# Four fused convolution layers on one core: the first batch's x in quarters of channels, weights on another queue, and reordered steps at the start, in the attention rounds and in the last blocks

## The chip, the core and the metric

The kernel runs on one core of a Trainium2 chip. TensorE (PE in the profile) does the matrix products, VectorE (DVE), ScalarE (ACT) and GpSimd (POOL) do the elementwise work, SyncE (SP) issues the transfers. The metric is the device time of one execution in microseconds. The kernel before takes 2680.13 us (median of three runs, 2679.41 to 2680.3). The profile used below is of one further execution, with a span of 2676.2 us on the core and a mean granted TensorE clock of 0.999.

## The reference, cut to what matters

An input x of shape (4, 512, 64, 64) in float32 goes through four layers, each of which adds to its input:

- layer 0, attention over the 4096 positions of an image with 64 channels: `scores = key^T query`, a softmax over the keys, `out = value @ attn`, then `scale * (w_out @ out) + x`. key, query and value are 1x1 convolutions of x by one weight array of 192 x 512.
- layer 1, a bottleneck of three convolutions (1x1, 3x3, 1x1) whose weights are mixed from eight experts; the mixing factors are a sigmoid of a linear map of the mean of layer 0's output.
- layer 2, linear attention: softplus features of Q and K, `KV = K V^T`, a division by a norm.
- layer 3, two projections of 512 to 512 channels; one is summed along columns and rows with a discount per channel, and the sigmoid of it multiplies the other.

The softmax in the kernel subtracts no maximum. The kernel collects the inverse sums of the exponentials and tests at run time that all lie in a range; a flag `fits` says so, and a slower general program behind a branch runs if they don't.

## The kernel before

**Tiling.** Channels are the 128 partitions in KC = 4 quarters. The 4096 positions are cut in four pieces of 1024 (a "pair" of two blocks of 512), and x[pr] holds all 512 channels of piece pr. All products are float32. The profile records a product of 512 columns as two matmul records; where two products of 64 output rows run side by side on the two halves of the array, as in most of layer 0, a group "x8" is two such pairs over two quarters.

**Start (L99 to L159).** SyncE issues the weights `wqkv` (L100, 128 x 4 pieces of 768 bytes), the parameters `prm` (L102), then x: pieces 0 and 1 in four transfers of one quarter of the channels each (L93, 512 KB), pieces 2 and 3 as one transfer each (L95, 2 MB). Up to eight transfers are under way at a time, because each uses one of eight semaphores in turn and the ninth waits for the first.

**First stage (`Projections`, L213 to L337).** TensorE's order is the program's order (the PE schedule is manual), and so is that of DVE and ACT in this stage. Pieces are taken in twos, (0, 1) and (2, 3). Keys and queries of the two pieces are made with seven products instead of eight (a Strassen-like scheme, numbered 1 to 7), written in the strings of `steps` (L230). What the words of a string mean:

- `v1`: the value product of piece 1 over all four quarters; `v3a`, `v3b` its halves.
- `1` to `7`: a product over two quarters (`kq`, `kqz`, L305); 1, 6, 7 and 4 accumulate in one bank, which is copied out on the way (`seed`, `e2`, `e3`, ACT, L310 and L313) or at the end (`c21`, DVE). 2 accumulates on the seed and needs channels 2 and 3 of the first piece only.
- `t5`, `n5` and so on: the sums of x that 4, 5, 6 and 7 need (DVE, L253), of this pair or the next.
- `c11` (ACT, L291): four copies of product 2's result to `key`. `c22`, `c12`: DVE additions into `qry` and `key`. `k`: the second copy of the keys that `c12` made.
- `cp01`, `tr01`: the values to SBUF (ACT), turned by TensorE, and copied (DVE).
- `zero`: a product of identities that has no use but to occupy the array and to clear a bank.

All products of one pair's scheme that go to `zy` share one PSUM tile; product 3 is written after `c11` and `c22` have read it. PSUM has three such double tiles (`pair_psum`) and two single banks (`bank`).

**Rounds (L458 to L481).** Attention goes over 128 steps i = (pr, kt), pr the query piece and kt the tile of 128 keys. A round g is eight `scores` (PE, L367, then the exponential on ACT, L370, and its sum into `acc` on DVE, L375) and eight `values` (PE, L382), which run four steps behind the scores. There are 16 rounds. `late` is a list of work for finished query pieces: `sums(pr)` is the sum over partitions (PE `den`, L398), its reciprocal (DVE, L401), the scaled result (L410, L412) and two range reductions (L419, L420); `out_step(pr, m)` is an output product (PE `y`, L426) and its addition to x (DVE, L431). At the end of each round up to two items of the list are taken:

```python
for _ in range(2):
    if late and late[0][0] <= g:
        late.pop(0)[1]()
```

For the last query piece `inverse_sums(3)` (`den` and its reciprocal) is put in by hand before the step `done == 121` of the values, seven before the end (L456).

**Layers 1 to 3.** Layer 1 mixes the weights and does `conv1` (L567), `sums_of_six`, `conv2` (L616), `conv3`. In layer 3 a `Block` is a set of seven products (L920); `Sums` blocks are summed along rows (`rows`, L953), turned (`turn`, ACT, L959), summed along columns (L970), and go through a sigmoid (L976); `Gates` blocks multiply by them, add x (L1015) and send the result out (L1017). The step tables `steps`, `last_steps` and, for the last two gates of the last batch, `end_steps` (L1037) say which step of which block comes when: s is the sums block, g and h the gates blocks, l the sums block before.

**Flag (L1114 to L1123).** After the last batch DVE reduces the collected inverse sums, TensorE adds up the partitions (`cnt`, L1122) and DVE casts the result to `fits` (L1123). Every engine then loads `fits` and branches (L1514, L1515).

Of the kernel before, what the change touches and what calls it, by code (L numbers as in the profile page):

```python
# [8 lines left out]
F32 = mybir.dt.float32  # L9
# [6 lines left out]
P = 128  # L16
# [5 lines left out]
D = 64  # L22
# [24 lines left out]
def unshifted(ctx: ExitStack, tc: tile.TileContext, fits, x, wqkv_t, wout_t, router_t,  # L47
# [16 lines left out]
    def bank(name, shape=(P, NB)):  # L64
        return ps.tile(list(shape), F32, tag="acc", name=name)
# [20 lines left out]
    def load_pair(b, pr):  # L86
        if b and pr == NPAIR - 1:
            places[NPAIR - 1:] = places[NPAIR], places[NPAIR - 1]
        t = places[pr]
        src = x[b, :, pr * 2 * NB:(pr + 1) * 2 * NB].rearrange("(kc p) n -> p kc n", p=P)  # L90
        if b == 0 and pr < 2:
            for kc in range(KC):
                nc.sync.dma_start(t[:, kc, :], src[:, kc, :])  # L93
        else:
            nc.sync.dma_start(t, src)  # L95
        return t


    wqkv_sb = const.tile([P, KC, 3 * D], F32, tag="wqkv", name="wqkv_sb")  # L99
    nc.sync.dma_start(wqkv_sb, wqkv_t.rearrange("(kc p) o -> p kc o", p=P))  # L100
    prm_sb = const.tile([P, NPRM], F32, tag="prm", name="prm_sb")
    nc.sync.dma_start(prm_sb, prm)  # L102
    def col(i, n=1):
        return prm_sb[:, i:i + n]

# [107 lines left out]
    class Projections:  # L213
# [14 lines left out]
            nc.vector.tensor_tensor(self.w[3], a12, self.w[6], ALU.subtract)  # L228

        def steps(self, b):  # L230
            first = "v1 cp01 5 1 seed v2 t6 t4 n5 6 n6 e2 2 7 e3 c22 c11 tr01 n7 4 c21 3 c12 n4"
            if b == 0:
                first = "zero v0 1 seed t5 v1 cp01 t6 5 2 t7 t4 6 e2 v2 7 e3 n5 c22 c11 tr01 n6 n7 4 c21 3 c12 n4"
            return first.split(), "5 1 seed k v3a 6 e2 2 v3b cp23 7 e3 c22 c11 tr23 4 c21 3 c12".split()

        def key_copies(self):
            while self.left:
# [44 lines left out]
        def products(self, xs, pair, steps, key, qry, vt):  # L282
            y = zy = None
            e = {}

            def to_key(src, pr, own=True):
                for h in range(2):
                    n0 = (2 * pr + h) * NB
                    for to in range(2):
                        if own or to != h:  # L290
                            nc.scalar.copy(key[to * D:(to + 1) * D, n0:n0 + NB], src(h, n0))  # L291

            for step in steps:
                if y is None and (step.isdigit() or step == "zero"):
                    y, zy = bank(f"kq_{self.b}_{pair[0]}"), pair_psum(f"kqz_{self.b}_{pair[0]}")
                if step == "zero":

                    nc.tensor.matmul(zy[:, 0, :].rearrange("p (j c) -> p j c", c=P), ident,
                                     ident[:, None, :].to_broadcast([P, TPB, P]), start=True, stop=True)
                elif step.isdigit():  # L300
                    k = int(step)
                    to = y if k in (1, 6, 7, 4) else zy[:, 0 if k == 2 else 1, :]
                    for c in range(2):
                        for h in range(2):
                            nc.tensor.matmul(to[h * D:(h + 1) * D, :], self.w[k][:, c, :],  # L305
                                             self.term(xs, pair, k, c)[:, h * NB:(h + 1) * NB],
                                             start=c == 0 and k in (1, 5), stop=c == 1,
                                             skip_group_check=k not in (1, 5))
                elif step == "seed":
                    nc.scalar.copy(zy[:, 0, :], y)  # L310
                elif step in ("e2", "e3"):
                    e[step] = block(f"{step}_{self.b}_{pair[0]}")
                    nc.scalar.copy(e[step], y)  # L313
                elif step == "c11":
                    to_key(lambda h, n0: zy[h * D:(h + 1) * D, 0, :], pair[0])
                elif step == "c12":
                    for h in range(2):
                        r, n0 = slice(h * D, (h + 1) * D), (2 * pair[1] + h) * NB
                        nc.vector.tensor_tensor(key[r, n0:n0 + NB], zy[r, 1, :], e["e2"][r, :], ALU.add)
                    self.left.append(lambda: to_key(lambda h, n0: key[h * D:(h + 1) * D, n0:n0 + NB], pair[1],  # L320
                                                    own=False))
                elif step == "k":
                    self.key_copies()
                elif step == "c21":
                    nc.vector.tensor_copy(qry[:, pair[0] * NB:(pair[0] + 1) * NB], y)
                elif step == "c22":
                    nc.vector.tensor_tensor(qry[:, pair[1] * NB:(pair[1] + 1) * NB], zy[:, 1, :], e["e3"], ALU.add)
                elif step[0] in "tn" and step[1].isdigit():
                    for c in range(2):
                        self.sum(xs, pair if step[0] == "t" else (2, 3), int(step[1]), c)  # L330
                elif step[:2] == "cp":
                    self.value_copy(int(step[2]) // 2)
                elif step[:2] == "tr":
                    self.value_turn(int(step[2]) // 2, vt)
                elif step[2:] == "a" or step[2:] == "b":
                    self.value(xs, int(step[1]), 0 if step[2] == "a" else 2, 2)
                else:  # L337
                    self.value(xs, int(step[1]))

    def layer0(b, xs, pro):  # L340
# [130 lines left out]
        assert not late  # L471


# [394 lines left out]
    def layer3(b, xs, value_product, value_add, left, weights, wcq):  # L868
# [109 lines left out]
        class Gates(Block):  # L978
# [32 lines left out]
            def add_x(self, i, h=None):  # L1011
# [25 lines left out]
        end_steps = (("s1", "s seed", "l rows 1", "l rows 0"), ("g1", "l turn 1", "g seed"),  # L1037
# [66 lines left out]
                    nxt.append(load_pair(b + 1, i // 2 - 1))  # L1104
        return nxt, pro

    with tc.manual_schedule(engines={mybir.EngineType.PE}):
# [7 lines left out]
    nc.vector.tensor_reduce(ends[:, 0:1], stat[:, 0, :], AX.X, ALU.add)  # L1115
    nc.vector.tensor_reduce(ends[:, 1:2], stat[:, 1, :], AX.X, ALU.min)
    fit = small.tile([P, 2], F32, tag="fit", name="fit", bufs=1)
    nc.vector.tensor_scalar(fit[:, 0:1], ends[:, 0:1], 1.0 / SUM_LO, None, ALU.is_le)
    nc.vector.tensor_scalar(fit[:, 1:2], ends[:, 1:2], 1.0 / SUM_HI, None, ALU.is_ge)
    nc.vector.tensor_tensor(fit[:, 0:1], fit[:, 0:1], fit[:, 1:2], ALU.mult)  # L1120
    cnt = bank("cnt", (1, 2))
    nc.tensor.matmul(cnt, fit[:, 0:1], ones[:, 0:2], start=True, stop=True)  # L1122
    nc.vector.tensor_copy(fits, cnt)  # L1123


@with_exitstack
def general(ctx: ExitStack, tc: tile.TileContext, x, wqkv_t, wout_t, router_t,
                experts, packed, wqk_t, wv_t, bv, wproj_t, prm, out):
# [23 lines left out]


    wqkv_sb = const.tile([P, KC, 3 * D], F32, tag="wqkv", name="wqkv_sb")
    nc.scalar.dma_start(wqkv_sb, wqkv_t.rearrange("(kc p) o -> p kc o", p=P))
# [411 lines left out]
```

## Time and profile before

| what | value |
|---|---|
| time, three runs | 2680.13 us (2679.41 to 2680.3) |
| span of the profiled execution | 2676.2 us, granted TensorE clock 0.999 |
| DVE busy | 2016.3 us (75%) |
| ACT busy | 1314.3 us (49%) |
| scores, L367 | 2048 records, 460.1 us busy |
| value products of the rounds, L382 | 1344 + 704 records, 302.2 + 159.6 us busy |
| layer 3 products, L920 | the chain of waits puts 14% on `sx` and 10% on `zy` |
| x's transfers, L95 | 14 of 2048 KB, 8.6 us to landing (median); the two of the first batch 14.6 and 19.3 us |
| x's transfers, L93 | 8 of 512 KB, 4.5 to 10.2 us to landing |

A row of the timeline has the start in us, the time from the first start to the last end of the merged instructions, the engine, the line, what is written and read, the number of records, and in brackets how long the engine was idle before and what ended it. The ends of matmuls are modelled, so that a group's printed time overlaps the next group's start; the differences of starts say what a group cost. In the list of waits a row has the total in us, how many times, and the longest.

### The profile page before, as it was taken

What the parts mean: (1) busy time and instruction counts of PE and PEld (TensorE: products, weight loads), DVE (VectorE), ACT (ScalarE), POOL (GpSimd) and SP (SyncE); (2) the same over time, 40 slices, a digit from 0 to 9 for tenths busy, and PEclk for the clock granted to TensorE, in tenths of its full rate; (3) what the DMA queues carried; (4) which work ended last, traced back from release to release, by engine and by line L of the source; (5) the groups of instructions that cost most, each with busy time, mean ns of one, the idle gap of its engine ahead of it and who ended that gap; (6) DMA issues with size and microseconds to landing.
All of it is one profiled execution on the core that took longest, in us unless ns stands there. A gap on an engine that the chain in (4) does not pass through costs nothing.

```text
span 2676.2 us, 25813 instructions
## 1 busy us (share of the span) xinstructions
PE 2643.2 (99%) x10048; PEld 1114.9 (42%) x10048; DVE 2016.3 (75%) x2272; ACT 1314.3 (49%) x1510; POOL 12.9 (0%) x26
## 2 busy tenths in 40 slices
PE   8999999999999999999999999999999999999998
PEld 2333364344333345434433334543443333554443
DVE  6777766788777776688877778668886777856787
ACT  3655353455555435345455553535555555263545
POOL 1000000000000000000000000000000000000000
PEclk9999999999999999999999999999999999999999
DMA  5000210022200021002220002101121000210001
GB/s 191 1 1 1 102 32 1 16 110 79 79 1 1 1 102 32 1 33 93 79 79 1 1 1 102 32 1 63 63 87 71 0 1 15 88 32 1 32 40 57
DMA packets 34883, 115.17 MB, mean 43 GB/s; under 512 B 3008, under 2 KB 12224, under 8 KB 33216
## 3 DMA queue, kind: packets, MB, share of 16 engines
q1 hardware_dynamic: 34752, 113.43, 11.4%
q8 instruction: 81, 1.33, 0.2%
q14 instruction: 50, 0.41, 0.1%
HBM read 79.86 MB, written 33.55 MB: 42 GB/s over the span
## 4 chain that ended last, share of the span: by engine, by line
PE 81%; DVE 11%; ACT 3%; issue 2%; DMA 1%; DVEq 0%; SPq 0%; ACTq 0%
PE av L382 14%; PE sx L920 14%; PE s L367 13%; PE zy L920 10%; DVE acc L375 4%; PE z L664 4%; PE c L639 4%; PE c L567 4%; PE c L616 3%; PE wv L838 2%; PE g L740 2%; PE xtr L725 2%; PE y L426 2%; PE c2e L616 2%; PE kqz L305 1%
## 5 line engine op out<-in xcount | busy, mean ns | idle before, releaser
L367 PE MATMUL s<-qv,key 64*128 64x512 f32 x2048 | 460.1, 596 | 0.9
L370 ACT ACTIVATE ring<-s 128x1024 f32<-128x1024 f32 x336 | 316.7, 1048 | 252.9 <-PE s L367 252.5
L375 DVE TENSOR_TENSOR acc<-acc,ring 128x1024 f32<-128x1024 f32 x312 | 381.7, 1223 | 59.2 <-ACT ring L370 31.3
L382 PE MATMUL av<-ring,qv 128*64 128x512 f32 x1344 | 302.2, 595 | 0.0
L367 PEld LDWEIGHTS s<-qv,key 64*128 64x128 f32 x2048 | 190.7, 186 | 265.3 <-issue 128.6
L920 PE MATMUL sx<-t,x 128*128 128x512 f32 x512 | 238.2, 599 | 2.2 <-ACT e L929 2.2
L375 DVE TENSOR_TENSOR acc<-acc,x 128x1024 f32<-128x1024 f32 x168 | 205.5, 1223 | 31.6 <-ACT x L370 15.5
L370 ACT ACTIVATE x<-s 128x1024 f32<-128x1024 f32 x176 | 167.1, 1053 | 124.9 <-PE s L367 124.6
L382 PEld LDWEIGHTS av<-ring,qv 128*64 128x64 f32 x1344 | 92.6, 137 | 200.1 <-issue 200.1
L925 ACT COPY zy<-sx 128x512 f32<-128x512 f32 x64 | 36.5, 570 | 258.0 <-PE sx L920 248.4
L382 PE MATMUL av<-x,qv 128*64 128x512 f32 x704 | 159.6, 595 | 0.0
L920 PEld LDWEIGHTS sx<-t,x 128*128 128x128 f32 x512 | 94.7, 190 | 134.1 <-issue 121.5
L970 DVE TENSOR_TENSOR_SCAN t<-x,t 128x512 f32<-128x512 f32 x128 | 149.2, 1209 | 1.6
L959 ACT COPY t<-s 128x1024 f32<-128x1024 f32 x64 | 127.6, 1993 | 43.9 <-DVE s L953 43.4
L953 DVE TENSOR_TENSOR_SCAN s<-wc,s 128x512 f32<-128x512 f32 x128 | 146.1, 1203 | 1.7 <-ACT s L945 1.7
L929 ACT ACTIVATE e<-sx,prm_sb 128x512 f32<-128x512 f32 x128 | 86.9, 686 | 107.0 <-PE sx L920 106.9
L976 ACT ACTIVATE s<-t 128x1024 f32<-128x1024 f32 x64 | 125.8, 1988 | 11.1 <-DVE t L970 11.1
L920 PE MATMUL zy<-t,wq 128*128 128x512 f32 x256 | 118.5, 602 | 0.5 <-ACT s L938 0.5
L920 PE MATMUL sx<-t,wq 128*128 128x512 f32 x256 | 117.0, 597 | 1.3 <-ACT e L929 1.3
L920 PE MATMUL sx<-x,wq 128*128 128x512 f32 x256 | 117.1, 595 | 0.0
L920 PE MATMUL zy<-x,x 128*128 128x512 f32 x256 | 116.3, 594 | 0.0
L920 PE MATMUL zy<-x,wq 128*128 128x512 f32 x256 | 115.9, 592 | 0.0
(227 smaller groups left out, 3451.1 us busy)
## 6 DMA issues: line engine op xcount, KB each, us to landing
out_dram<-s SPq DMA_DIRECT2D x62, 512.0 KB, 2.6
x<-in_x_dram SPq DMA_DIRECT2D x14, 2048.0 KB, 8.6
ex<-in_packed_dram SPq DMA_DIRECT2D x4, 2048.0 KB, 7.3
ex<-in_experts_dram SPq DMA_DIRECT2D x4, 2048.0 KB, 7.8
wq<-in_wproj_t_dram SPq DMA_DIRECT2D x32, 256.0 KB, 4.8
ex<-in_packed_dram SPq DMA_DIRECT2D x4, 1536.0 KB, 6.0
ex<-in_experts_dram SPq DMA_DIRECT2D x4, 1536.0 KB, 6.5
x<-in_packed_dram SPq DMA_DIRECT2D x4, 1536.0 KB, 7.6
```

The lines of the kernel that those rows point to most:

```text
L367: nc.tensor.matmul(s[:, h, :], key[r, kt * P:(kt + 1) * P], qry[r, pr * NB:(pr + 1) * NB], start=True, stop=True)
L370: nc.scalar.activation(p, s, AF.Exp)
L375: nc.vector.tensor_tensor(accs[pr], accs[pr], p, ALU.add)
L382: nc.tensor.matmul(avs[pr][h * D:(h + 1) * D, :], vt[:, kt, :], ring[i % RING][:, h, :], start=kt == 0, stop=kt == NT - 1)
L567: nc.tensor.matmul(y[:, h, :], wc[:, kc, :], xs[pr][:, kc, h * NB:(h + 1) * NB], start=kc == 0, stop=kc == KC - 1)
L616: nc.tensor.matmul(y[:, lo - a:hi - a], u, v[:, lo:hi], start=dy == 1, stop=dy == 2)
L639: nc.tensor.matmul(y[:, h, :], wc[:, KC + 9 + m, :], h2[:, h, :], start=True, stop=True)
L920: nc.tensor.matmul(y, w[:, c, self.kind, self.j * P:(self.j + 1) * P], v[:, c, :], start=c == 0 and k in (1, 5), stop=c == 1, skip_group_c ...
L953: nc.vector.tensor_tensor_scan(self.half(i, h), along[:, self.j + 2 * i, :], self.half(i, h), 0.0, ALU.mult, ALU.add)
L959: nc.scalar.copy(self.t[i].rearrange("p (w r) -> p w r", w=W), self.s[i].rearrange("p (r w) -> p w r", w=W))
L970: nc.vector.tensor_tensor_scan(th, down[:, i, :], th, 0.0, ALU.mult, ALU.add)
L976: nc.scalar.activation(self.s[i].rearrange("p (r w) -> p w r", w=W), tw, AF.Sigmoid)
```

## The change

It has six parts. They are meant to start TensorE earlier, to take waits off it, and to shorten the work after its last product.

1. All x of the first batch comes in quarters of channels, 16 transfers. `wqkv` and `prm` are issued by ACT instead of SyncE, and `wqkv` lies in memory as the tile does, 3072 bytes to a partition.
2. The identity product `zero` is done twice, and the first pair's products of the first batch follow the quarters as they come.
3. In all batches `c11` comes directly after product 2, and product 2 comes earlier; in the second pair `k` goes to the end.
4. One item of `late` per round instead of two; `inverse_sums(3)` five steps before the end instead of seven.
5. In `end_steps` the two turns of the last sums block come after the copies that the products wait for.
6. The range test is done in layer 1 of the last batch.

```diff
-        if b == 0 and pr < 2:
+        if b == 0:
             for kc in range(KC):
                 nc.sync.dma_start(t[:, kc, :], src[:, kc, :])
...
-    nc.sync.dma_start(wqkv_sb, wqkv_t.rearrange("(kc p) o -> p kc o", p=P))
+    nc.scalar.dma_start(wqkv_sb, wqkv_t)
     prm_sb = const.tile([P, NPRM], F32, tag="prm", name="prm_sb")
-    nc.sync.dma_start(prm_sb, prm)
+    nc.scalar.dma_start(prm_sb, prm)
...
-            first = "v1 cp01 5 1 seed v2 t6 t4 n5 6 n6 e2 2 7 e3 c22 c11 tr01 n7 4 c21 3 c12 n4"
+            first = "v1 cp01 5 1 seed v2a t6 2 c11 t4 n5 6 v2b e2 n6 7 e3 c22 tr01 n7 4 c21 3 c12 n4"
             if b == 0:
-                first = "zero v0 1 seed t5 v1 cp01 t6 5 2 t7 t4 6 e2 v2 7 e3 n5 c22 c11 tr01 n6 n7 4 c21 3 c12 n4"
-            return first.split(), "5 1 seed k v3a 6 e2 2 v3b cp23 7 e3 c22 c11 tr23 4 c21 3 c12".split()
+
+                first = ("zero v0:0 1:0 v0:1 1:1 seed v0:2 2:0 v0:3 2:1 c11 t5 v1:0 v1:1 5 t6 v1:2 v1:3 cp01 t7 6 e2 "
+                         "v2:0 v2:1 t4 7 e3 c22 tr01 n5 4 c21 n6 3 c12 n7 v2:2 v2:3 n4")
+            return first.split(), "5 1 seed v3a 2 c11 6 v3b e2 cp23 7 e3 c22 tr23 k 4 c21 3 c12".split()
...
-                    nc.tensor.matmul(zy[:, 0, :].rearrange("p (j c) -> p j c", c=P), ident,
-                                     ident[:, None, :].to_broadcast([P, TPB, P]), start=True, stop=True)
+
+                    for _ in range(2):
+                        nc.tensor.matmul(zy[:, 0, :].rearrange("p (j c) -> p j c", c=P), ident,
+                                         ident[:, None, :].to_broadcast([P, TPB, P]), start=True, stop=True)
...
-                    if done == NPAIR * NT - 7:
+                    if done == NPAIR * NT - 5:
                         inverse_sums(NPAIR - 1)
...
-                for _ in range(2):
-                    if late and late[0][0] <= g:
-                        late.pop(0)[1]()
+                if late and late[0][0] <= g:
+                    late.pop(0)[1]()
...
-        end_steps = (("s1", "s seed", "l rows 1", "l rows 0"), ("g1", "l turn 1", "g seed"),
-                     ("s6", "s copy_out 2", "l columns 1"), ("s2", "l turn 0", "s first"),
-                     ("s7", "s copy_out 3", "l columns 0", "l sigmoid 1"), ("s5", "s fourth"),
+        end_steps = (("s1", "s seed", "l rows 1", "l rows 0"), ("g1", "g seed"),
+                     ("s6", "s copy_out 2", "l turn 1", "l columns 1"), ("s2", "s first"),
+                     ("s7", "s copy_out 3", "l turn 0", "l columns 0", "l sigmoid 1"), ("s5", "s fourth"),
...
+    def all_in_range():
+
+        ends = small.tile([P, 2], F32, tag="ends", name="ends", bufs=1)
...
             convs = layer1(b, xs, *layer0(b, xs, pro))
+            if b == B - 1:
+                all_in_range()
             xs, pro = layer3(b, xs, *layer2(b, xs, *convs))
-
-
-    ends = small.tile([P, 2], F32, tag="ends", name="ends", bufs=1)
...
-        "wqkv_t": a["L0_conv_w_qkv"].T,
+
+        "wqkv_t": a["L0_conv_w_qkv"].T.reshape(KC, P, 3 * D).transpose(1, 0, 2),
```

In the order in which the instructions stand after building, `den` and the reciprocal of query piece 2 come at the end of round 12 in the kernel before, ahead of the sums of round 13 on DVE; in the changed kernel they come at the end of round 14, ahead of the sums of round 15, the last. What belongs to the general program is left out of the diff.

More of the change, by code (lines that the diff above doesn't have):

```diff
@@ L293, in products @@
             for step in steps:
+                step, _, channels = step.partition(":")
                 if y is None and (step.isdigit() or step == "zero"):
@@ L302, in products @@
                     to = y if k in (1, 6, 7, 4) else zy[:, 0 if k == 2 else 1, :]
-                    for c in range(2):
+                    for c in (int(channels),) if channels else range(2):
                         for h in range(2):
@@ L334, in products @@
                     self.value_turn(int(step[2]) // 2, vt)
+                elif channels:
+                    self.value(xs, int(step[1]), int(channels), 1)
                 elif step[2:] == "a" or step[2:] == "b":
@@ L1105, in layer3 @@
         return nxt, pro
+    def all_in_range():
+        ends = small.tile([P, 2], F32, tag="ends", name="ends", bufs=1)
+        nc.vector.tensor_reduce(ends[:, 0:1], stat[:, 0, :], AX.X, ALU.add)
+        nc.vector.tensor_reduce(ends[:, 1:2], stat[:, 1, :], AX.X, ALU.min)
+        fit = small.tile([P, 2], F32, tag="fit", name="fit", bufs=1)
+        nc.vector.tensor_scalar(fit[:, 0:1], ends[:, 0:1], 1.0 / SUM_LO, None, ALU.is_le)
+        nc.vector.tensor_scalar(fit[:, 1:2], ends[:, 1:2], 1.0 / SUM_HI, None, ALU.is_ge)
+        nc.vector.tensor_tensor(fit[:, 0:1], fit[:, 0:1], fit[:, 1:2], ALU.mult)
+        cnt = bank("cnt", (1, 2))
+        nc.tensor.matmul(cnt, fit[:, 0:1], ones[:, 0:2], start=True, stop=True)
+        nc.vector.tensor_copy(fits, cnt)
     with tc.manual_schedule(engines={mybir.EngineType.PE}):
@@ L1110, in unshifted @@
             convs = layer1(b, xs, *layer0(b, xs, pro))
+            if b == B - 1:
+                all_in_range()
             xs, pro = layer3(b, xs, *layer2(b, xs, *convs))
-    ends = small.tile([P, 2], F32, tag="ends", name="ends", bufs=1)
[L1115 to L1123, printed above, removed]
 @with_exitstack
@@ L1154, in general @@
     wqkv_sb = const.tile([P, KC, 3 * D], F32, tag="wqkv", name="wqkv_sb")
-    nc.scalar.dma_start(wqkv_sb, wqkv_t.rearrange("(kc p) o -> p kc o", p=P))
+    nc.scalar.dma_start(wqkv_sb, wqkv_t)
     xs = load_x(0)
```

## The prediction

> **What bounds the kernel now.** I read the page first, then TensorE's waits, then the timelines around each wait.
>
> ```profile
> PE 2643.2 (99%) x10048; PEld 1114.9 (42%) x10048; DVE 2016.3 (75%) x2272; ACT 1314.3 (49%) x1510; POOL 12.9 (0%) x26
> ```
>
> TensorE is the bound: 33 us of the span are left outside its busy time, and the change takes away no product. What it can win is in these 33 us, and in slow stretches that count as busy. TensorE's waits (total, times, longest) say where:
>
> ```profile
> PE kqz L305 <- ACT key L291: 8.4, 8, 1.6
> PE den L398 <- DVE acc L375: 5.0, 4, 1.2
> PE vv L261 <- DMA x<-in_x_dram: 3.6, 2, 2.9
> PE sx L920 <- ACT e L929: 3.6, 9, 1.4
> ```
>
> The first is product 3 behind the copies `c11`, twice a batch; the second is the last `den` of each batch; the third the start; 1.4 us of the fourth lie in the last blocks. The start, TensorE alone (start, length, records):
>
> ```profile
> 1.46 2.08 PE L298 MATMUL kqz<-ident 128*128 128x512 f32 x2 [1.46 <-POOL ident masks.py:199]
> 6.41 1.97 PE L261 MATMUL vv<-x,wqkv_sb 128*64 128x512 f32 x4 [2.87 <-DMA x<-in_x_dram]
> 9.10 4.87 PE L261 MATMUL vv<-x,wqkv_sb 128*64 128x512 f32 x12 [0.71 <-DMA x<-in_x_dram]
> 13.79 1.88 PE L305 MATMUL kq<-x,wqkv_sb 128*64 128x512 f32 x8
> ```
>
> The last row's group costs 1.72 us start to start (the next starts at 15.51). The sixteen value records from 6.41 to 13.79 cost 7.38 us where 2 x 1.72 = 3.44 would do: 3.9 us lost to arrivals and to a slow array. The first stage's end, TensorE, then ACT:
>
> ```profile
> 48.83 1.94 PE L305 MATMUL kq<-ring,wqkv_sb 128*64 128x512 f32 x8
> 51.67 1.94 PE L305 MATMUL kqz<-x,kqw 128*64 128x512 f32 x8 [0.90 <-ACT key L291]
> 53.53 0.70 PE L367 MATMUL s<-qv,key 64*128 64x512 f32 x2
> ```
>
> ```profile
> 49.26 2.35 ACT L291 COPY key<-kqz 64x512 f32<-64x512 f32 x4 [0.76 <-DVE qv L327]
> ```
>
> Product 4 to product 3 takes 2.84 us instead of 1.72: 1.1 us. The first pair (30.36 to 33.92) loses 1.8.
>
> [...] the work begun at 9.10 reaches 0.43 us per pair of records only at about 13.4, after 4.3 us; before, pairs are about 0.86 us apart. The windows view gives a clock of 1.00 throughout, so only the spacing shows it. [...] SyncE issues x from 1.79 us on, after 1.04 us of weights and parameters. [...]
>
> **Part by part.**
>
> *Start of batch 0 (parts 1, 2).* x's first quarter is issued at 0.75 instead of 1.79 and, at 4.5 us from issue to landing (the fastest in the trace), lands near 5. The weights go beside it; they landed 3.2 us after issue. The two identity products take 2 x 2.1 us from 1.46, to 5.6: they keep the array busy until x is there, so most of the slow time falls on work without use. Then TensorE has per quarter of piece 0 a value half and a product half, 4 x 0.43 = 1.72 us, against 1.27 us that 512 KB need at the 413 GB/s of the window 13.4 to 20. So it is no longer starved: sixteen quarters need 20.3 us and are in by 25 or 26, against 28.4 now (9.07 + 19.3), and piece 3 is first needed by the sums `n5`, on DVE at about 26. Work from 5.6 on: four values of 3.43, fourteen products of 1.72, two turns of 1.0, about 0.4 of changes of shape = 40.3, with 0.7 for a rest of slow clock [...] and 0.4 for small waits. Scores then begin at 47.0 instead of 53.5: **-6.5**, of which 1.8 + 1.1 are `c11` and 3.6 the start. Between -4 and -8.
>
> *`c11` in batches 1 to 3 (part 3).* Six waits of 1.1 go: **-6.4**, if nothing takes their place. Queued behind `c11` on ACT is `e2`, and product 7 waits for it: 2.35 + 0.58 + 0.1 us of latency = 3.05 after product 2, while TensorE does product 6 and a value half, 3.43 us. It fits by 0.4 us. `seed` (0.57) must end before product 2: a value half of 1.72 lies between. `c22` ends with about 1 us to spare before product 3. `k` moves into ACT's idle time before the first exponential (3.1 us idle in the trace). Both ends: -5 and -6.6.
>
> *One item per round (part 4).* Output products now come one to a round. In the rows below two of them and the scores behind:
>
> ```profile
> 137.39 1.99 PE L426 MATMUL y<-o,wout_sb 64*128 64x512 f32 x8
> 139.21 7.43 PE L367 MATMUL s<-qv,key 64*128 64x512 f32 x32
> ```
>
> The scores cost 7.36 us, start to start, instead of 7.07 in other rounds, because the third score wants the PSUM tile that DVE's second addition (two of 1.28) still reads; the other such rounds cost 7.26. With one item the addition ends 2.6 us after the output product's start, when the third score is due. Per batch: before 4 x 1.82 + 2 x 7.36 + 2 x 7.26 + 4 x 7.07 = 64.8; after 8 x 0.96 (a lone `den` costs that) + 8 x 6.97 (one change of shape of 0.1 less) = 63.4. -1.35; with small waits -1.15, times 4 **-4.6** (-3.5 to -5.4).
>
> But the reciprocal of query piece 2 moves from the end of round 12 to that of round 14, just ahead of the last round's sums. What it does to sums behind it is in the trace, after round 12. TensorE in rounds 12 and 15:
>
> ```profile
> 244.99 1.03 PE L398 MATMUL den<-acc,ones 128*64 128x512 f32 x4
> ...
> 274.12 7.14 PE L367 MATMUL s<-qv,key 64*128 64x512 f32 x32
> 281.19 4.51 PE L382 MATMUL av<-ring,qv 128*64 128x512 f32 x20
> 286.93 1.08 PE L398 MATMUL den<-acc,ones 128*64 128x512 f32 x4 [1.24 <-DVE acc L375]
> ```
>
> ```profile
> 246.06 3.36 DVE L401 RECIPROCAL rec<-den 128x512 f32<-128x512 f32 x1 [2.71 <-PE den L398]
> ...
> 253.53 7.87 DVE L375 TENSOR_TENSOR acc<-acc,ring 128x1024 f32<-128x1024 f32 x6
> ```
>
> There the eight sums end at 253.53 + 7.87 = 261.4, 15.45 us after the scores began (245.95). In round 15 now they end 12.8 after (286.9 - 274.12). So the last `den` becomes possible 2.7 us later. Moving it two steps back hides 2 x 0.86: its place is at 7.07 + 7 x 0.86 + 0.05 = 13.1 after the scores' start, it waits until 15.5. Then 0.91 for `den` and five values, 4.4: the values end at 20.8. Before they end at 293.95 - 274.12 = 19.8. Its own reciprocal ends at 20.0, before the values. **+1.0** a batch, **+3.9** in all (+3 to +5). The wait moved from 7 to 5 before the end would be gone if the reciprocal had not come in front of the sums.
>
> *Last blocks (part 5).* ACT, then TensorE:
>
> ```profile
> 2634.22 1.99 ACT L959 COPY t<-s 128x1024 f32<-128x1024 f32 x1 [2.79 <-DVE s L953]
> ...
> 2656.16 1.96 ACT L976 ACTIVATE s<-t 128x1024 f32<-128x1024 f32 x1
> ```
>
> ```profile
> 2637.36 1.98 PE L920 MATMUL sx<-t,x 128*128 128x512 f32 x4 [1.39 <-ACT e L929]
> ```
>
> The turn of 2 us stands ahead of the copies that product 7 wants: TensorE loses 1.4 + 0.5 us. But the end is set by DVE: from 2658.15, when the last sigmoid ends, it works without a pause to 2670.59. So only an earlier sigmoid counts. Following the queues with the durations of the trace: the first turn runs 2634.9 to 2636.9, the row sums of the last block begin at 2643.65 instead of 2644.28, its second turn at 2648.95 instead of 2650.02, the sigmoid at 2654.8 instead of 2656.16: **-1.4** (-0.7 to -1.9).
>
> *Flag (part 6).* The cast leaves the final DVE run (-0.1), `cnt` costs TensorE 0.3 in layer 1; its inputs are ready at 2311.7, long before `conv1` ends at 2323.6, so it waits for nothing. The branch after the end stays. **+0.2**.
>
> Sum: -6.5 - 6.4 - 4.6 + 3.9 - 1.4 + 0.2 = -14.8, so **2665.3 us**.
>
> **Rivals.** *A, the last den's wait is gone:* if DVE caught up in round 15, the values would end at 13.1 + 0.9 + 4.4 = 18.4, 1.4 earlier than now instead of 1.0 later: 2.4 x 4 less, 2655.7. Against it is the measured 15.45; for it, only that DVE has idle time in most rounds. 12%. *B, the start stays starved:* between the first and second value of x lie 2.7 us, twice a quarter's time; [...] the start wins 1 instead of 3.6 and `c11` and the rounds win at their lower ends: -3.9 - 5.0 - 3.5 + 3.9 - 0.7 + 0.2 = -9.0, 2671. 20%. *C, new waits, slower:* `c11` ahead of `e2` holds product 7 for what product 3 waited, the start wins nothing, output products each cost the change of shape without freeing the scores (+0.4 x 4), and `den` costs 5: 2680.1 + 1.6 + 5 + 0.2 = 2687. Against it: the 0.4 us of room, and 0.43 us per pair that waits don't change. 3%. The forecast has 65%.
>
> **How the numbers follow.** The forecast's own bounds give about 2661 to 2670. The range goes to 2658 and 2671: B nearly within, A left out, with C. Faster by over 0.2% (5.4 us) are the forecast, A and nearly all of B, 0.94; within 0.2% a worse B, 0.03; slower 0.03.
>
> **What would show it.** Scores of batch 0 start at 47 (right) or after 50 (start wrong). The row `kqz <- key` is gone from TensorE's waits. `den <- acc` is larger than 5.0, near 9 (mine), or gone (A). Scores behind an output product cost about 7.0. From the last sigmoid's end to the last DVE instruction's end it stays at 12.4 us. A wait of `kq` for `e` would be C. I'd be wrong most if DVE's order in round 15 costs less than in round 13.

## The result and the profile after

The changed kernel takes 2669.31 us (median of six executions, 2664.41 to 2669.94), the kernel before, on the same chip, 2679.89 us (2678.67 to 2680.30). The ratio is 0.9958, with a 95% interval from 0.9945 to 0.9971: faster by 0.42%. 2665.3 us had been predicted, between 2658 and 2671. The direction is right and the time lies in the range, but four microseconds are missing, and one step of the prediction lost more than these four.

The first lines of the page after, TensorE's busy time, and then the answer on TensorE's waits (total, times, longest):

```profile
PE 2642.4 (99%) x10050; PEld 1119.3 (42%) x10050; DVE 2016.2 (76%) x2272; ACT 1312.9 (49%) x1510; POOL 12.1 (0%) x26
```

```profile
PE den L405 <- DVE acc L382: 8.8, 4, 2.2
PE sx L926 <- ACT e L935: 2.1, 8, 0.3
...
PE vv L263 <- DMA wqkv_sb<-in_wqkv_t_dram: 0.8, 1, 0.8
PE kqz L310 <- ACT key L293: 0.8, 1, 0.8
```

The wait of `kqz` for `key` has shrunk from 8.4 us to one wait of 0.8, the start waits 0.8 us instead of 3.6, and the last blocks have lost their one long wait. `den` behind `acc` has grown from 5.0 to 8.8, "near 9" as predicted. TensorE's busy time, however, has fallen by only 0.8 us, although slow work at the start is gone and scores behind a lone output product take less time: something else has become slower while busy. The mean granted clock of TensorE says the same: 0.996 in this execution, 0.999 in the profiled one of before.

The start and the end of the first stage, timeline of TensorE after (start, length, records):

```profile
1.46 3.78 PE L303 MATMUL kqz<-ident 128*128 128x512 f32 x4 [1.46 <-POOL ident masks.py:199]
6.09 1.08 PE L263 MATMUL vv<-x,wqkv_sb 128*64 128x512 f32 x4 [0.85 <-DMA wqkv_sb<-in_wqkv_t_dram]
7.00 1.03 PE L310 MATMUL kq<-x,wqkv_sb 128*64 128x512 f32 x4
...
15.73 1.94 PE L310 MATMUL kqz<-ring,wqkv_sb 128*64 128x512 f32 x8 [0.80 <-ACT key L293]
...
45.59 1.89 PE L310 MATMUL kqz<-x,kqw 128*64 128x512 f32 x8
47.41 7.14 PE L374 MATMUL s<-qv,key 64*128 64x512 f32 x32
```

From 6.09 on each group of four records costs 0.86 to 0.91 us, which is full speed, and no product waits for x. The scores begin at 47.41 us; before, at 53.53; 47.0 was predicted.

The last round of the first batch, TensorE and then DVE:

```profile
266.35 7.14 PE L374 MATMUL s<-qv,key 64*128 64x512 f32 x32
273.42 6.23 PE L389 MATMUL av<-ring,qv 128*64 128x512 f32 x28
281.86 1.72 PE L405 MATMUL den<-acc,ones 128*64 128x512 f32 x4 [2.21 <-DVE acc L382]
283.36 1.93 PE L389 MATMUL av<-ring,qv 128*64 128x512 f32 x4
285.07 3.86 PE L389 MATMUL av<-x,qv 128*64 128x512 f32 x16
288.86 1.99 PE L433 MATMUL y<-o,wout_sb 64*128 64x512 f32 x8
```

```profile
266.47 3.36 DVE L408 RECIPROCAL rec<-den 128x512 f32<-128x512 f32 x1 [1.18 <-PE den L405]
...
276.60 5.21 DVE L382 TENSOR_TENSOR acc<-acc,x 128x1024 f32<-128x1024 f32 x4
```

The reciprocal stands ahead of the sums, the sums end at 276.60 + 5.21 = 281.8, and `den` starts at 281.86, 15.51 us after the scores; 15.5 was predicted. What follows was not predicted: `den` takes 283.36 - 281.86 = 1.50 us for four records instead of 0.91, and the next four values 1.71 instead of 0.86. That is half speed. The values end 288.86 - 266.35 = 22.51 us after the scores' start, not 20.8.

The last sigmoid and the product behind the first turn, ACT and then TensorE:

```profile
2647.06 1.95 ACT L982 ACTIVATE s<-t 128x1024 f32<-128x1024 f32 x1
```

```profile
2628.03 1.88 PE L926 MATMUL sx<-t,x 128*128 128x512 f32 x4
```

The wait of 1.39 us ahead of that product is gone.

With the starts of TensorE's groups in both traces as landmarks, the difference of the spans (2676.2 to 2667.4, -8.8 us) divides as follows. The gain of the medians is larger, 10.6, because the profiled execution of before was a short one: an execution's time is about 1.9 us above its span (2669.27 and 2667.4 for the one profiled here), so its time was some 2678.1 by this estimate, against the median of 2679.89.

| stretch | predicted | measured |
|---|---|---|
| start of batch 0, up to its first scores | -6.5 | -6.1 |
| first stage of batches 1 to 3 | -6.4 | -7.2 (-2.25, -2.46, -2.48) |
| rounds, without the last round's scores, `den` and values | -4.6 | -5.5 |
| last round, scores' start to the values' end | +3.9 | +10.7 (19.83 to 22.51, four times) |
| flag | +0.2 | +0.3 |
| last blocks | -1.4 | -1.05 |
| sum | -14.8 | -8.8 |

### The profile page after: what moved, and what is told of

Its sections match the earlier page's. It is cut to its first block, busy times and chain, and to the rows that moved or that the text cites. A ratio compares the mean times of both kernels' runs of the same rounds, so it can differ in the third digit from the quotient of the medians.

```text
span 2667.4 us, 25807 instructions
## 1 busy us (share of the span) xinstructions
PE 2642.4 (99%) x10050; PEld 1119.3 (42%) x10050; DVE 2016.2 (76%) x2272; ACT 1312.9 (49%) x1510; POOL 12.1 (0%) x26
## 4 chain that ended last, share of the span: by engine, by line
PE 91%; DVE 5%; ACT 2%; issue 1%; DMA 0%; DVEq 0%; ACTq 0%
PE av L389 16%; PE s L374 16%; PE sx L926 15%; PE zy L926 10%; PE z L670 4%; PE c L645 4%; PE c L573 4%; PE c L622 3%; PE y L433 2%; PE wv L844 2%; PE kq L310 2%; PE vv L263 2%; PE g L746 2%; PE xtr L731 2%; PE kqz L310 2%; PE c2e L622 2%
## 5 line engine op out<-in xcount | busy, mean ns | idle before, releaser
L374 PE MATMUL s<-qv,key 64*128 64x512 f32 x2048 | 453.9, 593 | 0.0
```

The lines of the kernel that those rows point to most:

```text
L374: nc.tensor.matmul(s[:, h, :], key[r, kt * P:(kt + 1) * P], qry[r, pr * NB:(pr + 1) * NB], start=True, stop=True)
```

## The experiments

Two explanations of the slow `den` stood against each other: the wait makes the array slow (T), or the records are slow because of something that runs beside them at that moment (W). The runs were made in three groups, in which the kernel before took 2679.05 us (experiments 1 to 3 and 5), 2677.34 (4 and 6 to 8) and 2678.28 (9 to 11). So a difference of one or two us between medians of different groups shows nothing by itself, and is read from the traces.

### 1. The sums of query piece 2 back at the end of round 12

```diff
-                        late.append((g, lambda pr=pr: sums(pr)))
+                        if pr == NPAIR - 2:
+                            at_once = pr
+                        else:
+                            late.append((g, lambda pr=pr: sums(pr)))
...
                 if late and late[0][0] <= g:
                     late.pop(0)[1]()
+                if at_once is not None:
+                    sums(at_once)
+                    at_once = None
```

> Changed kernel with the sums and the reciprocal of query piece 2 put back to the end of round 12 (beside that round's output product); all else one item a round. Theory T (DVE in the last round makes den wait, and the wait of 2.4 us lets the array fall to half speed, which costs another 1.6 us a batch): no wait, no slow stretch, the values end 18.4 us after the last round's scores begin instead of 22.5, 4 x 4.1 less: about 2653. Rival W (the wait alone; the slow records after den come from something that stays): 4 x 2.4 less, about 2660. Rival N (den waits for other work on DVE): about 2669.

2655.99 us (2654.97 to 2657.06), ratio to the kernel before 0.9914 (0.9897 to 0.9930): 13.3 us less than the changed kernel, and faster than both kernels. The same stretch of its timeline of TensorE:

```profile
267.03 7.14 PE L374 MATMUL s<-qv,key 64*128 64x512 f32 x32
274.10 6.23 PE L389 MATMUL av<-ring,qv 128*64 128x512 f32 x28
280.16 1.03 PE L405 MATMUL den<-acc,ones 128*64 128x512 f32 x4
281.02 1.03 PE L389 MATMUL av<-ring,qv 128*64 128x512 f32 x4
281.87 3.60 PE L389 MATMUL av<-x,qv 128*64 128x512 f32 x16
285.41 1.99 PE L433 MATMUL y<-o,wout_sb 64*128 64x512 f32 x8
```

No wait and no slow record, and a mean granted clock of 0.999 again; the values end 18.38 us after the scores' start, where rival A of the prediction had put them (18.4). The last round gains 22.51 - 18.38 = 4.13 us a batch; round 12, with two items again, gives 0.6 of it back, so a batch gains 3.53. The place of these sums on DVE, of which the reciprocal of 3.36 us is the longest part, is the cause of wait and slow stretch together. It does not tell T from W, since both went at once.

### 2. Two items per round, `den` five steps before the end

```diff
-                if late and late[0][0] <= g:
-                    late.pop(0)[1]()
+                for _ in range(2):
+                    if late and late[0][0] <= g:
+                        late.pop(0)[1]()
```

> Changed kernel with two items of the list a round as before, den still five steps before the end. T: the den wait and the slow stretch go (-16.4), the output products cost again what they did (+1.3 x 4): about 2658. W: -9.6 + 5.1, about 2665. If one item a round is what made the gain: slower than 2669.

2660.12 us (2658.76 to 2661.18), 0.9926 (0.9909 to 0.9943). The wait of `den` is gone here too. Against experiment 1 the rounds are longer by 0.69, 1.04, 0.69 and 0.69 us a batch; as experiment 1 itself takes two items in round 12 and pays 0.6 for it, one item in every round is worth about 1.3; the scores behind two output products cost 7.36 and 7.26 us, behind one 6.96 to 7.01. But of the 6.1 us between the spans of the two profiles 2.1 lie in the start: in this execution the array ran at half speed from 6.07 to 10.5 us, although the start of the two kernels is the same. Another 0.9 lie behind the last batch's rounds and stay unexplained. The start is not the same in every execution.

### 3 and 4. Useless products in place of the wait: too many, and the right number

Before each batch's last `den`, products of `ones` and x go to the bank that `den` then overwrites; the result stays the same. Five iterations first, then three:

```diff
             den = bank(f"den_{b}_{pr}")
+            if pr == NPAIR - 1:
+                for _ in range(5):
+                    for h in range(2):
+                        nc.tensor.matmul(den[h * D:(h + 1) * D, :], ones[:, 0:D], xs[0][:, 0, h * NB:(h + 1) * NB],
+                                         start=True, stop=True)
```

> Changed kernel with five pairs of useless products (2.15 us, into den's bank, which den overwrites) ahead of the last den, where TensorE waits 2.4 us. T: den starts when it did, but the records after it are 0.43 us a pair apart instead of 0.84: 4 x 1.6 less, about 2663. W: the products take the place of the wait and nothing else changes: about 2669.

2670.8 us (2669.7 to 2671.98), 0.9968 (0.9956 to 0.9979). The expectation had a mistake of size: five iterations are 20 records of 0.215 us, 4.3 us, not 2.15, and so 1.9 us longer than the wait. `den` came 1.9 us later, with no slow records, and the values ended only 0.16 us later than in the changed kernel. That spoke for T, but a run of the right size was needed.

> The changed kernel with three iterations of the useless products ahead of each batch's last den: 12 records at 0.215 us = 2.58 us, against the 2.4 us that TensorE waits there (five iterations, run before, overfilled by 1.9 us). The result of the kernel is not touched. Theory T (the array falls to half speed in the wait and stays there 2.6 us and more): no wait for den left, den's four records cost about 0.86 and the value records 0.43 a pair; values end 1.5 us earlier a batch than in the changed kernel, 6 in all: 2663.3 us. Rival W (the records after den are slow for another reason, such as DVE or ACT using the same memory at that moment): den stays at 1.5 and the values at 1.7 per four records, 2669.5 to 2670 us.

2663.92 us (2662.45 to 2665.76), 0.9951 (0.9934 to 0.9967). T's number was 2663.3, W's 2669.5 to 2670. Timeline of TensorE:

```profile
266.15 7.14 PE L374 MATMUL s<-qv,key 64*128 64x512 f32 x32
...
279.27 2.74 PE L407 MATMUL den<-x,ones 128*64 128x512 f32 x12
281.85 1.03 PE L410 MATMUL den<-acc,ones 128*64 128x512 f32 x4
282.71 1.03 PE L389 MATMUL av<-ring,qv 128*64 128x512 f32 x4
283.56 3.60 PE L389 MATMUL av<-x,qv 128*64 128x512 f32 x16
287.10 1.99 PE L438 MATMUL y<-o,wout_sb 64*128 64x512 f32 x8
```

`den` starts at the same moment as in the changed kernel (15.7 us after the scores instead of 15.5), ACT and DVE do the same beside it, and yet its four records take 0.86 us. W has fallen: only the idleness ahead of them has changed. The values end after 20.95 us.

### 5. One identity product instead of two at the start

```diff
-                    for _ in range(2):
+                    for _ in range(1):
```

> Changed kernel with one identity product at the start instead of two. T (the second one keeps the array busy, so that it is at full speed when x lands): the first pairs of records are 0.86 us apart for 3 to 4 us, scores of batch 0 start 1.5 to 2 us later, about 2671. Rival (x's arrival sets the start, the array's speed doesn't count): scores start at 47.4 as before, 2669.

2669.64 us (2668.76 to 2671.57), 0.9963 (0.9949 to 0.9977). In its profile the array is slow from 5.87 to 11.24 us and batch 0's scores begin at 49.84 instead of 47.41: 2.4 us. The median is only 0.3 us above that of the changed kernel. As the place of the slow stretches differs between executions (experiment 10), one profile of each does not settle what the second identity product is worth on average.

### 6. `c11` late again, on top of experiment 1

```diff
-            first = "v1 cp01 5 1 seed v2a t6 2 c11 t4 n5 6 v2b e2 n6 7 e3 c22 tr01 n7 4 c21 3 c12 n4"
+            first = "v1 cp01 5 1 seed v2a t6 2 t4 n5 6 v2b e2 n6 7 e3 c22 c11 tr01 n7 4 c21 3 c12 n4"
...
-            return first.split(), "5 1 seed v3a 2 c11 6 v3b e2 cp23 7 e3 c22 tr23 k 4 c21 3 c12".split()
+            return first.split(), "5 1 seed v3a 2 6 v3b e2 cp23 7 e3 c22 c11 tr23 k 4 c21 3 c12".split()
```

> The kernel with early sums, with the key copies c11 put back behind c22 in seven of the eight pairs (both of batches 1 to 3 and the second of batch 0). Theory T (product 3 waits 1.1 us behind c11 each time): 7 x 1.1 = 7.7 us more than the kernel with early sums (2656.0), 2663.7 us, the row of kqz waiting for key has 8 entries and about 8.5 us. Rival R (what c11 in front of e2 costs product 7 was nearly the same): under 2 us more, 2656 to 2658.

2664.51 us (2663.19 to 2665.6), 0.9951 (0.9934 to 0.9968): 8.5 us more than experiment 1; 7.7 was expected. Waits of TensorE:

```profile
PE kqz L310 <- ACT key L293: 8.3, 8, 1.8
```

One of the eight, of 0.8 us, is that of product 5 in batch 0, which stays; the seven others come to 7.5. By landmarks the first stages of batches 1 to 3 lose 3.17, 2.25 and 2.47 us, batch 0's second pair 0.92. The early `c11` costs product 7 nothing: there was no wait behind `e2` in the changed kernel.

### 7. Weights and parameters from SyncE again, on top of experiment 1

```diff
-    nc.scalar.dma_start(wqkv_sb, wqkv_t)
+    nc.sync.dma_start(wqkv_sb, wqkv_t)
...
-    nc.scalar.dma_start(prm_sb, prm)
+    nc.sync.dma_start(prm_sb, prm)
```

> The kernel with early sums, with weights and parameters issued again by SyncE ahead of x (the new layout stays). Theory T (weights on ACT's queue beside x landed 2.1 us later than alone, and that, not x, sets the start): weights land near 4.0, the first quarter of x near 6.3 or a little later, the first value starts at 6.3 to 6.6 instead of 6.1 and no later quarter is waited for, since quarters come every 1.28 us and are used every 1.72: scores of batch 0 at 47.7 to 48.0, 2656.3 us. Rival Q (the queue is worth its 1.04 us of issue): first value at 7.1, scores at 48.5, 2657.0 us. Rival F (weights issued first leave x alone on the engines, so x is no later): first value below 6.0, scores at 47.2, 2655.7.

2657.30 us (2656.43 to 2657.87), 0.9924 (0.9908 to 0.9941). Timeline of TensorE:

```profile
7.45 1.08 PE L263 MATMUL vv<-x,wqkv_sb 128*64 128x512 f32 x4 [2.20 <-DMA x<-in_x_dram]
8.33 1.06 PE L310 MATMUL kq<-x,wqkv_sb 128*64 128x512 f32 x4
```

The first value starts at 7.45 instead of 6.17, batch 0's scores 1.3 us later than in experiment 1, and the time is 1.3 us longer: rival Q, the queue is worth its issue time of 1.04 us and a little more. The new layout of the weights stays in both kernels, so what it is worth is not shown. My theory that x is hardly earlier through the second queue has fallen. Beside x the weights do land later (6.05 us in the changed kernel instead of 3.97 before), and now they set the start; it is a gain all the same, since x alone would have come later than that.

### 8. Product 5 of batch 0 behind all of piece 1's values, on top of experiment 1

```diff
-                first = ("zero v0:0 1:0 v0:1 1:1 seed v0:2 2:0 v0:3 2:1 c11 t5 v1:0 v1:1 5 t6 v1:2 v1:3 cp01 t7 6 e2 "
+                first = ("zero v0:0 1:0 v0:1 1:1 seed v0:2 2:0 v0:3 2:1 c11 t5 v1:0 v1:1 v1:2 v1:3 cp01 5 t6 t7 6 e2 "
```

> The kernel with early sums, and in batch 0 product 5 of the first pair behind all four value quarters of piece 1 instead of behind two. Theory T (product 5 waits 0.8 us because c11 still reads the PSUM tile that it writes to): the wait is gone, scores of batch 0 at 46.7 instead of 47.5, 2655.2 us. Rival M (the wait moves: product 6 follows product 5 at once, and its sums t6, or the copies of the values, are not ready): scores stay at 47.3 or later, 2656 us.

2654.15 us (2653.38 to 2654.52), 0.9912 (0.9895 to 0.9928), the lowest median of all; but the ratio does not set it apart from experiment 1's 0.9914, and the trace has to tell. Timeline of TensorE:

```profile
13.14 3.60 PE L263 MATMUL vv<-x,wqkv_sb 128*64 128x512 f32 x16
16.57 1.89 PE L310 MATMUL kqz<-ring,wqkv_sb 128*64 128x512 f32 x8
18.29 1.89 PE L310 MATMUL kq<-ring,kqw 128*64 128x512 f32 x8
```

The wait of 0.8 us is gone and did not move elsewhere; scores of batch 0 begin 1.0 us earlier, which is the gain that is shown.

### 9. A third of the filling: a wait of 1.5 us stays

The wait of 1.24 us in the kernel before was followed by full speed (`den` 0.91 us), the wait of the changed kernel was not. The trace's record of the granted clock, which the windows view prints as PEclk, places the slow stretches of the changed kernel:

| | clock 0.50 from | to |
|---|---|---|
| batch 0 | 282.16 | 285.58 |
| batch 1 | 944.35 | 947.76 |
| batch 2 | 1606.54 | 1609.95 |
| batch 3 | 2268.72 | 2272.13 |

Around the first of them, the windows view (stretch and its length, busy time of PE, PEld, DVE, ACT and POOL, then PEclk, DMA share and GB/s):

```profile
278.75:282.16 3.41, 1.20 (x8) 0.21 (x6) 2.85 (x3) 0.00 (x0) 0.00 (x0) 1.00 0.02 7
282.17:285.57 3.40, 3.40 (x10) 0.98 (x8) 1.95 (x1) 0.00 (x0) 0.00 (x0) 0.50 0.00 0
285.59:289.00 3.41, 3.41 (x18) 1.00 (x16) 1.41 (x2) 0.00 (x0) 0.00 (x0) 1.00 0.68 213
```

The spacing of the records agrees: a pair costs 0.43 us at full speed and 0.85 in the slow stretch. (At the start of a kernel the view prints 1.00 also where pairs are 0.85 apart, as from 9.10 to 13.3 us in the kernel before; there the spacing decides, as the prediction says.) Each stretch lasts 3.41 us, and none begins with the wait or with its end: `den` starts at 281.86, 944.10, 1606.33 and 2268.59, and the clock falls 0.13 to 0.30 us later. The wait of batch 0 lasts 2.39 us by the spacing, from 279.47 (the end of the value pair begun at 279.05) to 281.86.

To see what a wait only a little longer than that of the kernel before does (1.24 us by modelled ends), one iteration of the useless products (4 records, 0.86 us) was put ahead of `den`, in the changed kernel:

```diff
+                for _ in range(1):
```

> The changed kernel with one iteration of the useless products ahead of each batch's last den: 4 records, 0.86 us, so that a wait of about 1.5 us stays. The result is not touched. Theory G [...] den and the values run at full speed although TensorE still waits: values end 20.9 us after the scores' start, about 2663.5 us, as with three iterations. Rival H (every wait longer than the 1.24 us of the kernel before slows the array): a slow stretch stays, values end at 22.3 or later, 2669 us.

2663.3 us (2662.02 to 2664.86), 0.9941 (0.9926 to 0.9957). Waits and timeline of TensorE:

```profile
PE den L410 <- DVE acc L382: 5.4, 4, 1.4
```

```profile
268.37 7.14 PE L374 MATMUL s<-qv,key 64*128 64x512 f32 x32
...
283.88 1.08 PE L410 MATMUL den<-acc,ones 128*64 128x512 f32 x4 [1.36 <-DVE acc L382]
284.79 1.03 PE L389 MATMUL av<-ring,qv 128*64 128x512 f32 x4
```

TensorE still waits, four times 1.4 us (1.53 by the spacing of the records), and all four batches run at full speed behind it. The values end 20.81 us after the scores' start in each. That is the prediction's 20.8, with `den` still at 15.51. Filling a third of the wait is as good as filling all of it: what was lost beyond the forecast was not the wait, but the slow stretch behind it.

Experiment 6 has a longer wait that did no harm. In its batch 1 TensorE waits for `c11` (timeline, then the windows view of the stretch behind):

```profile
692.27 1.94 PE L310 MATMUL kqz<-x,kqw 128*64 128x512 f32 x8 [1.83 <-ACT key L293]
```

```profile
692.36:695.70 3.34, 3.34 (x16) 1.11 (x18) 2.90 (x4) 1.16 (x1) 0.00 (x0) 1.00 0.02 5
```

By the spacing of the records TensorE is idle for 2.0 us here. Behind it the groups of eight records cost 1.71 to 1.77 us, and the clock stays at 1.00.

### 10. The changed kernel once more

> The changed kernel once more, unaltered, for the spread of its executions. Theory G [...]: in some executions [...] all four batches keep full speed[...]; the times then fall into two groups, about 2669.5 (five of the six so far) and about 2663 to 2664.5 (one, 2664.41)[...]. Rival H (a wait of this length always slows the array): all times within 1 us of 2669.5, and the 2664.41 was chance of another kind.

2669.11 us (2667.58 to 2669.47), 0.9964 (0.9950 to 0.9978). Not two groups, but steps: with the first six, seven executions lie between 2669.1 and 2669.9, three between 2667.6 and 2668.0, and one at 2664.4. The profile, of an execution of 2667.99 us, shows what a step is. Its batches 0 and 1, timeline of TensorE:

```profile
281.98 1.08 PE L405 MATMUL den<-acc,ones 128*64 128x512 f32 x4 [2.21 <-DVE acc L382]
282.89 1.03 PE L389 MATMUL av<-ring,qv 128*64 128x512 f32 x4
283.75 3.60 PE L389 MATMUL av<-x,qv 128*64 128x512 f32 x16
```

```profile
942.54 1.51 PE L405 MATMUL den<-acc,ones 128*64 128x512 f32 x4 [2.21 <-DVE acc L382]
943.83 1.93 PE L389 MATMUL av<-ring,qv 128*64 128x512 f32 x4
945.54 4.07 PE L389 MATMUL av<-x,qv 128*64 128x512 f32 x16
```

The same wait of 2.21 us in the same kernel: full speed after it in batch 0, half speed in batch 1. The values end after 20.81 us in batch 0 and after 22.51 in the others. In batch 1 the clock falls at 943.05, 0.51 us after `den` has started. What sets batch 0's wait apart from the others, no trace shows. My expectation had all four batches of an execution at full speed together; here one is and three are not. H, which has a wait of this length always slow the array, is refuted by these six lines. By steps of 1.7 us, the execution of 2664.41 would have had three batches at full speed (2669.5 - 3 x 1.7 = 2664.4); no trace of it exists, so that is an inference. Its mean granted clock, 0.998 where the ten others have 0.996 or 0.997, says only that it had fewer slow stretches; four batches at full speed behind a slow start would fit the time as well.

### 11. The old order of the last blocks, on top of experiment 8

```diff
-        end_steps = (("s1", "s seed", "l rows 1", "l rows 0"), ("g1", "g seed"),
-                     ("s6", "s copy_out 2", "l turn 1", "l columns 1"), ("s2", "s first"),
-                     ("s7", "s copy_out 3", "l turn 0", "l columns 0", "l sigmoid 1"), ("s5", "s fourth"),
+        end_steps = (("s1", "s seed", "l rows 1", "l rows 0"), ("g1", "l turn 1", "g seed"),
+                     ("s6", "s copy_out 2", "l columns 1"), ("s2", "l turn 0", "s first"),
+                     ("s7", "s copy_out 3", "l columns 0", "l sigmoid 1"), ("s5", "s fourth"),
```

> The kernel with early sums and product 5 later (2654.15 us), with the old order of the last blocks. Theory T (the last sigmoid, and with it the end, comes 1.3 us later, as the first turn of the last rows stands ahead of the copies that product 7 wants): 2655.5 us, TensorE's wait of sx for e back to 3.6 us in total. Rival N (the end is set by DVE's queue from earlier on, and the order on ACT is hidden): 2654.1 us.

2657.19 us (2654.73 to 2657.79), 0.9918 (0.9903 to 0.9933): 3.0 us more, where 1.4 was expected. Of these, 1.6 are a slow start of the profiled execution (to 9.4 us), which has nothing to do with the edit; from the last landmark of layer 2 to the end of the span it is 1.28 longer. Waits of TensorE:

```profile
PE sx L932 <- ACT e L941: 3.5, 9, 1.4
```

The ninth wait, of 1.4 us, is back. T's size is confirmed by the trace; the median alone could not have told it.

## Why the prediction was right, and where its sum was wrong

**Start of batch 0: right.** -6.1 for -6.5. Both halves held: no product waited for a quarter, and the slow time fell on the identity products, at least in this execution. Three details were not foreseen. The weights, not x, gate the start, at 6.05 us; product 5 waits 0.8 us for `c11` in the shared PSUM tile (experiment 8); and full speed at the first value does not come in every execution: with the same start, scores of batch 0 began at 49.6 and 49.4 us in the profiles of experiments 2 and 9. The range of -4 to -8 was needed.

**`c11`: right.** -7.2 for -6.4. The difference is one of size: six times 1.1 is 6.6, and the six waits listed in the trace of before, 0.90 to 1.14 us each by modelled ends, come to 7.1 with the 0.2 that the modelled ends hide. The room of 0.4 us ahead of product 7 was enough; undoing it cost 7.5 us of waits in seven pairs (experiment 6).

**One item per round: right.** The eight rounds with output products cost 64.80 us before and 63.45 after (8 x 0.96 + 2 x 7.00 + 6 x 6.96), -1.35 a batch, the very number of the prediction; the small waits taken off it (0.2) did not come. Experiments 1 and 2 together have about 1.3 for it.

**Last `den`: mechanism right, size wrong.** This is the step that failed. The prediction read off the reciprocal's new place, the end of the sums at 15.45 us and `den` at 15.5, and all that came to 0.1 us. Then it wrote "Then 0.91 for `den` and five values, 4.4", with 0.91 taken from a row behind a wait of 1.24 us. Behind the longer wait the array ran at half speed for 3.41 us: +1.7 a batch. Instead of +1.0 a batch, +2.7 was measured; 4 x 1.7 = 6.8 us. Of these `c11` and the rounds gave 0.8 + 0.9 back, start, tail and flag took another 0.9, which makes the 6.0 between the two sums of the table. With the wait only shortened to 1.5 us the prediction's 20.8 appears (20.81, experiment 9), and its time would have been 2663 to 2664, close to the 2665.3 forecast. The prediction had read slow pairs of 0.86 us at the start from the trace, but held that waits don't change the 0.43 us of a pair, and did not doubt this for a wait that it had itself worked out, 13.1 to 15.5 us after the scores' start, as longer than any behind the start. Behind that wait pairs cost 0.85 us.

**Last blocks and flag: right.** The last sigmoid, taken from where layer 2 leaves off, came 1.3 us earlier (-1.4 predicted), of which 0.3 went again after the last DVE instruction; experiment 11 has 1.28. The flag cost 0.3; no experiment took it, or `den`'s move from seven to five steps before the end, out alone.

**The rivals.** The time is nearer to rival B's 2671 than to the forecast, but B's reason, a starved start, did not occur. Rival A's number for the last round was what the kernel does when the reciprocal is kept out of it (experiment 1). C's waits, of product 7 for `e2`, never came. That the time still fell into the range was in part luck. The last `den` and values left their own bounds of +3 to +5 by 5.7 us; the range held because `c11` and the rounds gained 1.7 more than forecast, and because it reached up to 2671 for rival B, which did not occur. The bounds given for the parts, added up, reach from 2661 to 2672, not to 2670 as the prediction says.

## What to carry to other kernels

When a change lengthens a wait of the bounding engine, price what comes after the wait as well: here 2.4 us of idleness cost another 1.7 us of slow products in seven of eight traced waits, and twelve useless records, or only four, bought that back. Better is to ask what the waiting instruction waits for and to move work that nobody needs yet from in front of it: the sums of one query piece, with a reciprocal of 3.4 us, put two rounds earlier, were worth 13 us, more than the whole change. And where times of one kernel come in steps, compare traces by landmarks before comparing medians.

## What was not expected of the hardware

- In two profiles of the changed kernel, seven of the eight waits of 2.39 us by the spacing of the records (2.21 by modelled ends) ahead of `den` were followed by half speed. The eighth (experiment 10, batch 0) was not, nor were the four waits of 1.53 us in experiment 9, one of 2.0 us in experiment 6, or the four of 1.24 us by modelled ends in the kernel before. The length of the wait alone does not tell, and what else decides, these traces do not show.
- The slow stretch begins not with the wait but after work has resumed, 0.13 to 0.30 us behind the start of `den` in the changed kernel's profile and 0.51 us behind it in batch 1 of experiment 10. In the changed kernel's profile it lasts 3.41 us each time.
- From one `den` to the next batch's lie 662.24 us when a slow stretch follows the first (281.86 to 944.10 in the changed kernel's profile) and 660.56 us when none does (281.98 to 942.54 in experiment 10). What a kernel with another period would see, no run shows.
- Reaching full speed at the start varies between executions of the same start: before the first value (5.7 us) in the changed kernel's profile, at 9.4 to 10.5 us in those of experiments 2, 9 and 11. It is worth 1.6 to 2.1 us. What decides it is not shown.
